# A gated-linear-attention and expert kernel: tokens normalized two tiles at a time, the second output product, its store and the decay sums a step later

## The chip, the core and the metric

The kernel runs on one core of a Trainium2 chip. The engines of the core are TensorE (PE: matmuls, with its weight loads as PEld), VectorE (DVE), ScalarE (ACT), GpSimd (POOL) and SyncE (SP, which here only issues DMAs). Each engine works through its own instructions in the order in which they stand; semaphores make one wait for another. Transfers are made by 16 DMA engines. The metric is the device time of one execution in microseconds (us), and of several runs the median.

## The reference

8192 tokens (4 sequences of 2048) of width 256 are normalized, and two branches are added to the tokens: linear attention with a decay for each head, and a mixture of 64 experts of which each token takes 8.

```python
xn = _layernorm(x, axis=-1)
# attention, 8 heads, DK = 128, DV = 64
q = (x @ Wq); k = (x @ Wk) * DK ** (-0.5); v = (x @ Wv)
alpha = sigmoid((x @ Wg + bg) / 16)
state = at[..., None, None] * state + kt[..., None] * vt[:, :, None, :]
out_t = einsum('bhk,bhkv->bhv', qt, state)
return out * sigmoid(x @ Wog) @ Wo
# experts: groups of 8, the best 4 groups, the best 8 experts, 256 places each
y = einsum('eci,eih->ech', silu(g) * u, w_down)
out = zeros((n, h)).at[token].add(y_slots * w_slot[:, None])
# result
x + attention(xn) + experts(xn)
```

Here `x` inside the two branches is `xn`.

## The kernel before

**Two halves.** Tokens are taken in 32 blocks of 256 (`NS`, two chunks of 128 each) for the attention, and in 16 batches of 512 (`NB`, four tiles of 128) for normalization and routing. A function `block(s)` writes out the attention of block s with twelve calls of `step()` between its parts. In `step()` the side work advances: generators in the list `side`, each with the step at which it starts, run to their next `yield`. In the first half (blocks 0 to 16) these are, one batch to a block, `front(b)` (normalize, part into two half-precision numbers, transpose, routing logits), `back(b)` (choice of experts) and, in groups of batches, `decays(gi)` (sums of the logarithms of the decays). When they are done, from block 17 on, `step()` advances the experts instead, 4.8 to a block: gathers of token rows by POOL (L599), three products, an accumulating scatter by POOL (L677).

**Who sets the order.** The program is written in the order that `block` and `step` give, but a scheduler then orders each engine's instructions by its own reckoning of when they can start. The order of the built program is therefore known, and it differs from the written one.

**A block.** With halves of four heads, block s computes, in the written order: `unit_a(s,0,0)` (the decay matrix: product lp, L864, two activations and the triangle `dc`, L874 on POOL; the scores `sp`), the query product of the second half q10 (`queries(s,1,0)`), the key product k10, then after a step `unit_d(s,0,0)` (product `od`, output `oT`, the new state), the two output products of the block before, here o0 and o1 (`output(s-1,0)` and `output(s-1,1)`, L943 to L947), a step, `finish(s-1)`, then `unit_a(s,0,1)` with its lp, the query product q11, and after a step the key product k11 and the gates (`wog`). Products in half precision are made of three matmuls each (L259, L260, L261): high by high, high by low, low by high. So each result is parted by ACT into a high half (`qh`, `k`, `oh`) and by another engine into a low half (`ql` and `k` at L211 on DVE; `ol` at L935, on POOL in the first half). `qt` (L835, DVE) multiplies a query product by `el`, the decay that SP loads; it is the last to read the query product. `kt` is the transpose of `k` by a DMA that SP issues (L854).

**PSUM.** The query, key, value, gate and output products and lp share one pool of banks, `pj`, taken in turn: 4 banks in the first half, 3 in the second. A product whose bank has not been read by all its readers waits. The routing logits `lg`, `cs`, `ep`, `ltp` and `cp` have the other pool, `mo`.

**front.** For batches from 2 on: statistics by DVE; `rstd` and `nb` by some 14 small POOL operations (L346 to L351); a step later four activations on ACT, one for each tile, in place in `xt` (L362); a step later one cast of all four tiles (L366, ACT) and one subtraction for the low half (L367, POOL), the transposing DMA into `xT` (L370), and the store of the rows (L373); a step later the spill of `xT`, the copy of x to the output and the next batch's load; six steps later `lg`.

**decays.** Logarithm; a step later the sum and its parting into two, `g` (L413, L414); a step later four matmuls for `cs` (L417 to L421), two exponentials and the parting of `cs` into three; a step later the transposes `ep` and `ltp` and the stores to `el_d` and `lt_d`, which later blocks load.

**finish.** For blocks before 17 POOL issues an accumulating DMA of the block's result `res` to the output (L953). From block 17 on ACT issues a plain store to `at_d` (L957), and after each group of blocks (`TOGETHER`: 17 to 20, 21 to 24, 25 to 28, 29 and 30) POOL issues one accumulating DMA of the whole group (L961), in turn with the experts' gathers and scatters.

Of the kernel before, what the change touches and what calls it, by code (L numbers as in the profile page):

```python
# [13 lines left out]
AF = mybir.ActivationFunctionType  # L14
ALU = mybir.AluOpType
# [15 lines left out]
RT = 4  # L31
# [40 lines left out]
def gla_moe_kernel(ctx: ExitStack, tc: tile.TileContext, x, Wq, Wk, Wv, Wo, Wg, bg, Wog,  # L72
                   gate_wT, gate_bias, w_gate, w_up, w_down, out):
    nc = tc.nc
# [239 lines left out]
    def front(b):  # L314

        rows = slice(b * RB, (b + 1) * RB)
        xt = batch[b].pop("xt")
        st = r2.tile([P, RT, 6], F32, name="st")
        mv = r2.tile([P, RT, 2], F32, name="mv")
        for t in range(RT):  # L320
            nc.vector.bn_stats(out=st[:, t, :], in_=xt[:, t, :])
        for t in range(RT):
            nc.vector.bn_aggr(out=mv[:, t, :], in_=st[:, t, :])

        va = r2.tile([P, RT], F32, name="va")
        nc.vector.tensor_scalar(va, mv[:, :, 1], EPS, XFIT ** -2, ALU.add, ALU.mult)
        yi = r2.tile([P, RT], I32, name="yi")
        nc.vector.tensor_scalar(yi, va.bitcast(I32), 1, None, ALU.logical_shift_right)
        rstd = r2.tile([P, RT], F32, name="rstd")
        nc.vector.tensor_scalar(rstd.bitcast(I32), yi, -1.0, float(0x5f3759df), ALU.mult, ALU.add)  # L330
        yield True
        nt = r2.tile([P, RT], F32, name="nt")
        nb = r2.tile([P, RT], F32, name="nb")
        x16 = r1.tile([P, RT, 2, D], F16, name="x16")
        flat = x16.rearrange("p t a d -> p t (a d)")
        xT = r2.tile([P, RT, 2, 2, P], F16, name="xT")
        if b < 2:
            for _ in range(3):
                nc.vector.tensor_tensor(nt, rstd, rstd, ALU.mult)
                nc.vector.scalar_tensor_tensor(nt, in0=nt, scalar=-0.5, in1=va, op0=ALU.mult, op1=ALU.mult)  # L340
                nc.vector.scalar_tensor_tensor(rstd, in0=nt, scalar=1.5, in1=rstd, op0=ALU.add, op1=ALU.mult)
            nc.vector.scalar_tensor_tensor(nb, in0=mv[:, :, 0], scalar=-1.0, in1=rstd,
                                           op0=ALU.mult, op1=ALU.mult)
        else:
            for _ in range(3):
                nc.gpsimd.tensor_tensor(nt, rstd, rstd, ALU.mult)  # L346
                nc.gpsimd.tensor_tensor(nt, nt, va, ALU.mult)
                nc.gpsimd.tensor_scalar(nt, nt, -0.5, 1.5, ALU.mult, ALU.add)
                nc.gpsimd.tensor_tensor(rstd, rstd, nt, ALU.mult)
            nc.gpsimd.tensor_tensor(nb, mv[:, :, 0], rstd, ALU.mult)  # L350
            nc.gpsimd.tensor_scalar(nb, nb, -1.0, None, ALU.mult)  # L351
        if b < 2:
            for t in range(RT):
                made["hi"] = nc.scalar.activation(x16[:, t, 0, :], xt[:, t, :], AF.Identity,
                                                  bias=nb[:, t:t + 1], scale=rstd[:, t:t + 1]).ins
                xn = t5.tile([P, D], F32, tag="t5", name="xn")
                nc.vector.tensor_scalar(xn, xt[:, t, :], rstd[:, t:t + 1], nb[:, t:t + 1], ALU.mult, ALU.add)
                made["xn"] = nc.vector.tensor_tensor(x16[:, t, 1, :], xn, x16[:, t, 0, :], ALU.subtract).ins
        else:
            yield True  # L360
            for t in range(RT):
                nc.scalar.activation(xt[:, t, :], xt[:, t, :], AF.Identity,  # L362
                                     bias=nb[:, t:t + 1], scale=rstd[:, t:t + 1])
            yield True

            nc.scalar.copy(x16[:, :, 0, :], xt)  # L366
            nc.gpsimd.tensor_tensor(x16[:, :, 1, :], xt, x16[:, :, 0, :], ALU.subtract)  # L367
        n = 2 if b == 0 else RT
        for t in range(0, RT, n):
            made["xT"] = nc.sync.dma_start(  # L370
                out=xT[:, t:t + n].rearrange("p t a c i -> p (t a c) i"),
                in_=flat[:, t:t + n].rearrange("p t k -> p (t k)"), transpose=True).ins
        nc.sync.dma_start(out=xw_d[rows, 0:D].rearrange("(t p) d -> p t d", p=P),  # L373
                          in_=flat.bitcast(F32))
        yield True
        stored = nc.sync.dma_start(out=xT_d[b], in_=xT)
        with tc.issue_after(stored.ins):
            nc.sync.dma_start(out=of[rows, :], in_=xf[rows, :])
        batch[b]["xT"] = xT
        if 0 < b < NB - 1:  # L380
            load_x(b + 1)
        for _ in range(6 if b > 2 else 1):
            yield True
        lg = ps["mo"].tile([P, RT, E + H], F32, tag="mo", name="lg")
        for t in range(RT):
            for c in range(2):
                made["lg"] = product(lg[:, t, :], (xT[:, t, 0, c, :], xT[:, t, 1, c, :]),
                                     (gwz[:, 0, c, :], gwz[:, 1, c, :]), c == 0, c == 1)
        nc.vector.scalar_tensor_tensor(zs[:, b].rearrange("p h t -> p t h"), in0=lg[:, :, E:E + H],
                                       scalar=unfit[:, WG:WG + 1], in1=bc(brow, 1, RT),  # L390
                                       op0=ALU.mult, op1=ALU.add)
        nc.scalar.activation(sg[:, b], zs[:, b], AF.Sigmoid)
        sc = r3.tile([P, RT, E], F32, name="sc")
        nc.scalar.activation(sc, lg[:, :, 0:E], AF.Sigmoid, scale=unfit[:, GATE:GATE + 1])
        batch[b]["sc"] = sc
        yield True

    def decays(gi):
# [14 lines left out]
        nc.vector.tensor_scalar(g[:, 0, :], z, CGRID, CGRID, ALU.add, ALU.subtract)  # L413
        made["g"] = nc.vector.tensor_tensor(g[:, 1, :], z, g[:, 0, :], ALU.subtract).ins  # L414
        yield True
        cs = ps["mo"].tile([P, 4, n], F32, tag="mo", name="cs")
        nc.tensor.matmul(cs[:, 0:2, :].rearrange("p a n -> p (a n)"), lhsT=u_le,  # L417
                         rhs=g.rearrange("p a n -> p (a n)"), start=True, stop=True)
# [26 lines left out]
        for i in range(nb_):  # L445
            b = b0 + i
# [437 lines left out]
    def unit_m(s, half, ck):  # L884
        B = blk[s]
        dc = B["dc", half, ck]
        anchor.append(nc.vector.tensor_tensor(dc, B["sp"], dc, ALU.mult).ins)  # L887
# [50 lines left out]
    def output(s, ck):  # L938
        B = blk[s]
        if ck == 0:  # L940
            B["res"] = w2.tile([P, NCK, D], F32, name="res")
        oh_, ol_ = B["oT"][ck]
        rp = ps["pj"].tile([P, D], F32, tag="pj", name="pj")  # L943
        for hp in range(4):
            product(rp, (oh_[:, hp, :], ol_[:, hp, :]),
                    (wparts["wo"][0][:, hp, :], wparts["wo"][1][:, hp, :]), hp == 0, hp == 3)
        nc.scalar.copy(B["res"][:, ck, :], rp)  # L947
# [26 lines left out]
    def block(s):  # L974


        n = s + 1 < NS
        if n:
            load_block(s + 1)
            load_el(s + 1, 0)  # L980
        unit_a(s, 0, 0)
        if n:
            queries(s, 1, 0)
        else:
            keys(s, 1, 0)
        unit_m(s, 0, 0)
        step()
        if n:
            keys(s, 1, 0)
        else:  # L990
            keys(s, 1, 1)
        step()
        unit_d(s, 0, 0)
        if s:
            output(s - 1, 0)
            output(s - 1, 1)
        step()
        if s:
            finish(s - 1)

        unit_a(s, 0, 1)
        queries(s, 1, 1 if n else 0)
        unit_m(s, 0, 1)
        step()
        if n:
            keys(s, 1, 1)
        else:
            queries(s, 1, 1)
        if n:
            load_el(s + 1, 1)  # L1010
            gate(s + 1, 0)
        step()
        unit_d(s, 0, 1)
        step()

        if not n:
            unit_a(s, 1, 0)
            unit_m(s, 1, 0)
            unit_a(s, 1, 1)
            unit_d(s, 1, 0)  # L1020
            split_o(s, 0)
            unit_m(s, 1, 1)
            output(s, 0)
            unit_d(s, 1, 1)
            split_o(s, 1)
            step()
            return
        unit_a(s, 1, 0)
        gate(s + 1, 1)
        unit_m(s, 1, 0)  # L1030
        step()
        values(s + 1, 0)
        queries(s + 1, 0, 0)
        step()
        unit_d(s, 1, 0)
        split_o(s, 0)
        step()

        unit_a(s, 1, 1)
        keys(s + 1, 0, 0)  # L1040
        unit_m(s, 1, 1)
        step()
        queries(s + 1, 0, 1)
        keys(s + 1, 0, 1)
        values(s + 1, 1)
        step()
        unit_d(s, 1, 1)
        split_o(s, 1)
        step()
# [140 lines left out]
```

## Time and profile before

| what | value |
|---|---|
| median of 3 runs | 1230.19 us (1227.66 to 1234.02) |
| profiled execution | 1224.75 us |
| its span, first to last instruction | 1223.0 us |
| mean granted TensorE clock | 0.989 |
| busy: PE, DVE, ACT, POOL | 1134.6, 957.4, 743.8, 725.2 us |
| PE busy from 160 to 200 us, from 640 to 680 us | 38.6 and 40.0 of 40 us |
| HBM | 143 GB/s over the span |

A name such as `pj<-xs,wq_h` says which tile an instruction writes and which it reads. In a list of waits a row tells who waited, who ended the wait, and the time in total, the times and the longest. In the timeline a row has the start, the length, the engine and line, the operation, the tiles, the shapes, and in brackets the idle time of the engine before it with what ended it. A busy PE is not a PE at its peak, since the ends of matmuls are modelled. Weight loads run beside matmuls.

### The profile page before, as it was taken

What the parts mean: (1) busy time and instruction counts of PE and PEld (TensorE: products, weight loads), DVE (VectorE), ACT (ScalarE), POOL (GpSimd) and SP (SyncE); (2) the same over time, 40 slices, a digit from 0 to 9 for tenths busy, and PEclk for the clock granted to TensorE, in tenths of its full rate; (3) what the DMA queues carried; (4) which work ended last, traced back from release to release, by engine and by line L of the source; (5) the groups of instructions that cost most, each with busy time, mean ns of one, the idle gap of its engine ahead of it and who ended that gap; (6) DMA issues with size and microseconds to landing.
All of it is one profiled execution on the core that took longest, in us unless ns stands there. A gap on an engine that the chain in (4) does not pass through costs nothing.

```text
span 1223.0 us, 32182 instructions
## 1 busy us (share of the span) xinstructions
PE 1134.6 (93%) x12409; PEld 959.4 (78%) x12421; DVE 957.4 (78%) x2631; ACT 743.8 (61%) x1394; POOL 725.2 (59%) x892
## 2 busy tenths in 40 slices
PE   3797999988898999999989999999999899999898
PEld 2576877777687787787768888888888788888787
DVE  7978777766678666767878898888889778888775
ACT  4567566666566666644546666656676556665564
POOL 4376677765576677653225665576665647665642
PEclk9999999999999999999999999999999999999899
DMA  7759777687676876655868889889788998988855
GB/s 232 208 138 239 168 178 173 174 170 163 138 176 166 183 181 150 150 104 126 177 120 174 177 178 187 203 179 202 175 198 166 186 156 173 188 177 175 193 77 95
DMA packets 315001, 207.14 MB, mean 169 GB/s; under 512 B 198816, under 2 KB 285728, under 8 KB 314144
## 3 DMA queue, kind: packets, MB, share of 16 engines
q1 hardware_dynamic: 281328, 155.52, 53.9%
q0 software_dynamic: 29712, 45.89, 22.5%
q10 hardware_dynamic: 3808, 3.67, 0.9%
q8 instruction: 97, 1.59, 0.5%
q14 instruction: 56, 0.46, 0.1%
HBM read 115.98 MB, written 58.38 MB: 143 GB/s over the span
## 4 chain that ended last, share of the span: by engine, by line
PE 52%; DVE 15%; DMA 13%; POOL 8%; ACT 6%; issue 4%; SPq 1%; POOLq 0%; DVEq 0%; ACTq 0%
PE pj L261 9%; PE pj L259 9%; PE pj L260 8%; DMA kt<-k 7%; PE od L904 3%; DMA el<-el_d 3%; PE od L908 2%; PE gu L259 2%; PE gu L260 2%; PE gu L261 2%; PE xet L619 2%; DVE qt L835 2%; DVE k L211 1%; ACT xt L362 1%; DVE ql L211 1%
## 5 line engine op out<-in xcount | busy, mean ns | idle before, releaser
L677 POOL DMA_INDIRECT out_dram<-y,idx x128 | 212.5, 1660 | 141.9 <-DMA out_dram<-y,idx 74.6
L599 POOL DMA_INDIRECT xe<-xw_d,idx x128 | 140.4, 1097 | 102.4 <-ACT y L663 31.7
L211 DVE SCALAR_TENSOR_TENSOR ql<-pj,qh 128x512 f16<-128x512 f32 x128 | 87.1, 681 | 68.3 <-ACT qh L210 68.2
L259 PE MATMUL pj<-xs,wk_h 128*128 128x256 f16 x496 | 135.9, 274 | 1.7 <-ACT og L802 1.7
L260 PE MATMUL pj<-xs,wk_h 128*128 128x256 f16 x496 | 135.6, 273 | 0.0
L261 PE MATMUL pj<-xs,wk_l 128*128 128x256 f16 x496 | 135.6, 273 | 0.0
L259 PE MATMUL pj<-xs,wq_h 128*128 128x256 f16 x496 | 135.3, 273 | 0.2 <-DVE k L211 0.2
L261 PE MATMUL pj<-xs,wq_l 128*128 128x256 f16 x496 | 135.3, 273 | 0.0
L260 PE MATMUL pj<-xs,wq_h 128*128 128x256 f16 x496 | 135.3, 273 | 0.0
L887 DVE TENSOR_TENSOR dc<-sp,dc 128x512 f32<-128x512 f32 x128 | 87.4, 683 | 39.2 <-POOL dc L874 31.2
L904 PE MATMUL od<-dc,v 128*64 128x128 f32 x1024 | 107.7, 287 | 7.4 <-DVE dc L887 6.5
L210 ACT ACTIVATE k<-pj 128x512 f16<-128x512 f32 x128 | 76.2, 596 | 43.5 <-PE pj L261 43.2
L210 ACT ACTIVATE qh<-pj 128x512 f16<-128x512 f32 x128 | 76.3, 596 | 40.1 <-PE pj L261 39.7
L908 PE MATMUL od<-qt,state 128*64 128x128 f32 x960 | 98.6, 274 | 0.0
L259 PE MATMUL sp<-qh,k 128*128 128x128 f16 x512 | 96.8, 223 | 0.7 <-ACT k L210 0.2
L261 PE MATMUL sp<-qh,k 128*128 128x128 f16 x512 | 96.4, 223 | 0.8 <-DVE k L211 0.6
L260 PE MATMUL sp<-ql,k 128*128 128x128 f16 x512 | 96.2, 222 | 0.4 <-DVE ql L211 0.4
L211 DVE SCALAR_TENSOR_TENSOR k<-pj,k 128x512 f16<-128x512 f32 x128 | 86.6, 677 | 6.7 <-ACT k L210 6.6
L917 DVE SCALAR_TENSOR_TENSOR oT<-og,od 128x256 f32<-128x256 f32 x128 | 52.9, 413 | 46.6 <-PE od L261 44.4
L663 ACT ACTIVATE y<-yp,xe 128x256 f32<-128x256 f32 x128 | 53.6, 470 | 58.3 <-PE yp L261 52.8
L835 DVE SCALAR_TENSOR_TENSOR qt<-pj,el 128x512 f32<-128x512 f32 x128 | 86.7, 678 | 1.5 <-DMA el<-el_d 1.5
L868 ACT ACTIVATE dc<-lp 128x512 f32<-128x512 f32 x128 | 76.5, 598 | 18.6 <-PE lp L864 16.8
(397 smaller groups left out, 4242.2 us busy)
## 6 DMA issues: line engine op xcount, KB each, us to landing
el<-el_d SPq DMA_DIRECT2D x64, 512.0 KB
xw_d<-x SPq DMA_DIRECT2D x16, 512.0 KB
xT_d<-xT SPq DMA_DIRECT2D x16, 512.0 KB
out_dram<-in_L_attn_x_dram SPq DMA_DIRECT2D x16, 512.0 KB
w<-in_L_ffn_w_gate_dram SPq DMA_DIRECT2D x64, 128.0 KB
w<-in_L_ffn_w_up_dram SPq DMA_DIRECT2D x64, 128.0 KB
w<-in_L_ffn_w_down_dram SPq DMA_DIRECT2D x64, 128.0 KB
xs<-xT_d SPq DMA_DIRECT2D x31, 256.0 KB
```

Source lines behind the costliest of these rows:

```text
L210: return (nc.scalar.activation(hi, t, AF.Copy, scale=scale).ins, nc.vector.scalar_tensor_tensor(lo, in0=t, scalar=scale, in1=hi, op0=ALU.m ...
L211: nc.vector.scalar_tensor_tensor(lo, in0=t, scalar=scale, in1=hi, op0=ALU.mult, op1=ALU.subtract).ins)
L259: nc.tensor.matmul(out_, lhsT=a[0], rhs=b[0], start=first, stop=False)
L260: nc.tensor.matmul(out_, lhsT=a[0], rhs=b[1], start=False, stop=False)
L261: return nc.tensor.matmul(out_, lhsT=a[1], rhs=b[0], start=False, stop=last).ins
L599: in_turn(lambda: nc.gpsimd.indirect_dma_start(out=xe[:, f, :], out_offset=None, in_=xw_d[:, :], in_offset=bass.IndirectOffsetOnAxis(ap=id ...
L677: two = [in_turn(lambda: nc.gpsimd.indirect_dma_start(out=of, out_offset=bass.IndirectOffsetOnAxis(ap=idx[:, e, f:f + 1], axis=0), in_=m[" ...
L835: read = nc.vector.scalar_tensor_tensor(qt, in0=pj, scalar=QFIT, in1=two_heads(el, i), op0=ALU.mult, op1=ALU.mult)
L868: nc.scalar.activation(dc, lp, AF.Relu, scale=-1.0)
L887: anchor.append(nc.vector.tensor_tensor(dc, B["sp"], dc, ALU.mult).ins)
L904: nc.tensor.matmul(op[i * DV:(i + 1) * DV, j, :], lhsT=v[:, h0 + 2 * j + i, :], rhs=dc[:, 2 * j + i, :], start=True, stop=first)
L908: nc.tensor.matmul(op[i * DV:(i + 1) * DV, j, :], lhsT=state[half][:, 2 * j + i, :], rhs=qt[:, ck, 2 * j + i, :], start=False, stop=True)
```

## The change

Four edits. In `front` the normalization goes two tiles at a time: in one step the activations of tiles 0 and 1, in the next those of tiles 2 and 3 together with the cast and the subtraction of tiles 0 and 1, in the third the cast and the subtraction of tiles 2 and 3, then the transposing DMA and the row store. Cast and subtraction are thus two instructions each instead of one, and all that follows them is a step later; `lg` stays in its step for batches from 3 on, because one of the six steps ahead of it goes. In `decays` a further step stands between `g` and `cs` for every group but the first. In `block` the second output product is made after the second `unit_m`, behind lp and q11, and `finish` after it.

```diff
         else:
-            yield True
-            for t in range(RT):
-                nc.scalar.activation(xt[:, t, :], xt[:, t, :], AF.Identity,
-                                     bias=nb[:, t:t + 1], scale=rstd[:, t:t + 1])
-            yield True
-
-            nc.scalar.copy(x16[:, :, 0, :], xt)
-            nc.gpsimd.tensor_tensor(x16[:, :, 1, :], xt, x16[:, :, 0, :], ALU.subtract)
+
+            for t in range(0, RT + 2, 2):
+                yield True
+                if t < RT:
+                    for t2 in range(t, t + 2):
+                        nc.scalar.activation(xt[:, t2, :], xt[:, t2, :], AF.Identity,
+                                             bias=nb[:, t2:t2 + 1], scale=rstd[:, t2:t2 + 1])
+                if t:
+                    ts = slice(t - 2, t)
+                    nc.scalar.copy(x16[:, ts, 0, :], xt[:, ts])
+                    nc.gpsimd.tensor_tensor(x16[:, ts, 1, :], xt[:, ts], x16[:, ts, 0, :], ALU.subtract)
...
-        for _ in range(6 if b > 2 else 1):
+        for _ in range(5 if b > 2 else 1):
             yield True
...
         yield True
+        if gi:
+            yield True
         cs = ps["mo"].tile([P, 4, n], F32, tag="mo", name="cs")
...
         if s:
             output(s - 1, 0)
-            output(s - 1, 1)
         step()
-        if s:
-            finish(s - 1)
 
         unit_a(s, 0, 1)
         queries(s, 1, 1 if n else 0)
         unit_m(s, 0, 1)
+        if s:
+            output(s - 1, 1)
+            finish(s - 1)
         step()
```

## The prediction

> **What bounds the kernel now.** I read the page first, then PE's waits, then the timeline where the longest of them end, then the transfers and the granted clock by stretch.
>
> The page's busy list:
>
> ```profile
> PE 1134.6 (93%) x12409; PEld 959.4 (78%) x12421; DVE 957.4 (78%) x2631; ACT 743.8 (61%) x1394; POOL 725.2 (59%) x892
> ```
>
> PE is the bound: 88 us of the span are idle, 34 of them in the first 120 us. The change adds no matmul, so it can only move PE's waits. The longest of them (who waited, us in total, times, longest):
>
> ```profile
> PE od L259 <- DMA kt<-k: 21.4, 9, 5.0
> PE lg L259 <- DMA xT<-x: 11.0, 3, 9.8
> PE pj L259 <- DVE qt L835: 10.3, 5, 3.8
> ...
> PE pj L261 <- POOL ol L935: 7.0, 7, 1.7
> ...
> PE cs L417 <- DVE g L414: 3.5, 3, 1.7
> ```
>
> The change aims at three of these: ol (block boundaries of the first half, tokens with routing), qt (the same half), cs. The timeline at a boundary (start, length, instruction, idle before it):
>
> ```profile
> 185.47 1.27 POOL L935 TENSOR_TENSOR ol<-oT,oh 128x512 fp32r<-128x512 f32 x1
> ...
> 186.71 0.68 DVE L835 SCALAR_TENSOR_TENSOR qt<-pj,el 128x512 f32<-128x512 f32 x1
> 186.79 0.39 PE L261 MATMUL pj<-wo_h,ol 128*128 128x256 f32 x1 [0.87 <-POOL ol L935]
> ```
>
> The second output product (o1) waits for POOL's low half; qt, 0.6 us behind, has no PE work waiting yet. Both long qt waits come from ACT:
>
> ```profile
> 322.82 2.07 ACT L362 ACTIVATE xt<-xt,nb,rstd 128x256 f32<-128x256 f32 x4 [2.08 <-POOL nb L351]
> 324.91 1.28 ACT L869 ACT_TABLE_LOAD   x1
> 326.21 0.63 ACT L869 ACTIVATE dc<-dc 128x512 f32<-128x512 f32 x1
> 326.74 0.58 ACT L210 ACTIVATE qh<-pj 128x512 f16<-128x512 f32 x1
> ```
>
> Four normalizations stand ahead of qh. PE, waiting for the pj bank that qt releases, sat idle for 3.82 us until 328.70. In the second half (experts) PE waits for kt alone:
>
> ```profile
> 941.66 0.93 POOL L961 DMA_DIRECT2D out_dram<-at_d  x1 [4.47 <-DVE le__16521 L586]
> ...
> 946.26 8.83 SPq L854 DMA_TRANSPOSE kt<-k  x1
> ...
> 960.23 0.24 PE L259 MATMUL od<-vwh,kt 128*128 128x64 f16 x1 [4.69 <-DMA kt<-k]
> ```
>
> **Second output product, first half.** In the order of the changed program's instructions o1 stands behind lp and the query product q11, so ol has 0.2 + 12 x 0.109 = 1.5 us more; the seven waits are 0.5 to 1.66, so the 7.0 go. But the four pj banks are taken in turn: before, o1 and lp lie between the query products q10 and q11, and lp takes q10's bank, a product later. Now the turn is q10, k10, o0, lp, q11, and q11 takes q10's bank, which qt releases last. At this boundary o0 starts at 184.01, its 12 matmuls of 0.117 and lp end at 185.65, and q11 waits until 187.45: 1.8 us in place of 0.87. From there q11 (1.31) and o1 (1.42) end at 190.18, against 189.63 before. At six boundaries qt's end less the end of the ol wait is 0.37, 0.60, 0.62, 0.10, 1.24 and 0.07 us: the new wait is about 1.5 each, 0.5 longer than the old. I charge 1.5 at twelve boundaries (blocks 3 to 14): +18. It is zero wherever qt is early, as at 15 and 16.
>
> **Two tiles at a time.** Each of 14 batches gets one more ACT cast and one more POOL subtraction. The nearest rows of half size are vwh and vwl (616 and 1216 ns) against 1037 and 2185 for the whole: 14 x 0.20 = 2.7 us of ACT and 14 x 0.25 = 3.5 us of POOL, hidden by idle shares of 39% and 41%; uncovered they would add at most those 6 us. What matters is order: in most blocks the built order still has the four normalizations together, but behind qh of q11, also where the two long waits were (3.16 and 3.82). In three blocks they stand ahead of qh; there q11 is earlier by o1 (1.4 us), and I leave 0.7 us each. All 10.3 us of qt waits go, and one stretch of half clock: 3.4 us at 0.50, so 1.7.
>
> The transposes, the row store, the spill, the copy of x and the next load come a step later on SP, in the old places relative to kt in most blocks. The next load has over six steps (some 16 us) against a transfer of about 5. Cost nothing; if a load were late, the front alone would slip.
>
> **Sums of log decays.** cs leaves the wait for g by standing behind a product: of 3.5 us 0.5 stay, and the 0.9 us wait of ltp behind it goes. Its DMAs to el_d and lt_d come a step later; block 8 first needs them at 316, they were stored from 255 on.
>
> **The store and the adds.** finish is behind o1. In the first half POOL's accumulate issue (1.28 us) waits for res behind ACT's normalizations, and the state product (L926) and the subtraction queue behind it. The state product ran at 161.00 for a DVE add at 166.89, so some 2 us later is covered; without cover each microsecond goes to the next block's od. In the second half the ACT-issued store and POOL's 1 MB add (L961, three of them, and one of half that size) move past lp and q11: 1.5 us. The gathers queued behind the add were issued 17 us or more before their use, so nobody waits. At the tail the last add waited for expert adds until 1209 anyway; a store landing 1.5 us later costs 0 to 1.
>
> What changes is the add's lead over kt. It was issued 4.6 us before kt at 941.66, and 3.2 us before kt at 1123.29. While it ran, the transfers by queue read:
>
> ```profile
> q0 software_dynamic: 211, 1.31, 87.4%
> q1 hardware_dynamic: 138, 0.28, 11.5%
> ```
>
> (stretch 943 to 951: packets, MB, share of 16 engines; kt is in q1). So kt waited for the add almost whole, and two waits of 4.69 and 4.98 came with 10.2 us of half clock, 5.1 lost: 14.8 in all are at stake. A lead shorter by 1.5 us lets el and the rest ahead of kt move before the add: I take 1.5 for each of the two, -3. The bounds are 0 and -14.8 (kt wholly ahead), and +1.5 each if the add merely ends later.
>
> The Trainium skill says otherwise of such a pair ("DMA: Bandwidth & Descriptors", Queues, rings and completion order): a DMA engine takes the queues it has work for in turn, a packet each. By that kt would share evenly, the lead would hardly matter, and this term would be 0. The 11.5% speaks against it here.
>
> **Sum.** Gone: ol 7.0, qt 10.3, cs and ltp 3.9, half clock 1.7, and of the 1.65 of block 16's wait for res all (that bank now comes from lp): 24.5. New: 18 + 2.1 for the three blocks = 20.1. First half -4.4; with -3 for the adds -7.4. The profiled execution took 1224.75 us (span 1223.0 and 1.75 around it), 0.4% under the median of 1230.19 (runs 1227.66 to 1234.02). Against its own time this is 1217.3; against the median, which I forecast, 1222.8.
>
> **The rivals.**
>
> *kt passes the adds.* From o1's end to the end of the key product before kt, PE has in the old order 7.2 and 7.7 us of work for the two waits, in the new 1.5 and 3.6. If the small difference lets kt go first, all 14.8 go instead of 3: 1211. Against it: el and xs are still ahead of kt in its queue. 0.16.
>
> *The wait only changes its name.* At the boundaries the chain table load, exp, qh, ql, qt is the limit, whichever PE instruction waits for it; if the long qt waits return as waits of lp or the gate and the adds stay, only cs and little else remains: -1.5, 1228.7. For it: 18 of 24.5 come back in my own sum. 0.24.
>
> *The bank wait decides, slower.* qt's chain begins with lg, which PE itself delivers, so a late PE makes the next qt late. If q11 waits 2.4 us, not 1.5, at the twelve boundaries, that is +11. It turns at 2.1 us a boundary, where the gain is gone. Waits of that size also reach the clock: the kt wait of 2.35 us at 983.28 was followed by a granted clock of 0.50, those for ol of 1.42 and 1.66 by none:
>
> ```profile
> 983.50:986.90 3.40, 3.40 (x31) 3.31 (x28) 1.58 (x5) 0.68 (x2) 2.27 (x2) 0.50 0.55 155
> 415.00:421.00 6.00, 4.58 (x38) 4.11 (x37) 2.58 (x4) 4.00 (x8) 4.24 (x13) 1.00 0.44 93
> ```
>
> (stretch, its length, busy time of the five engines, granted clock.) With four such stretches at 1.7 it is +18 in all: 1241. 0.20.
>
> The skill ("TensorE: Matmul & The Clock Gate", Part 1) has the clock halved only after an idle window of some 3.4 us; by it the last 7 us would not come. The stretch after 983.28 disagrees.
>
> **How the numbers follow.** My forecast has 0.40, and within it 1215 to 1228. 0.5%, 6.15 us, is about what a measurement can tell from no change: faster means under 1224.0. Of the forecast 0.31 lies there, with the first rival 0.47; the second rival and 0.09 of the forecast give 0.33; the third 0.20. The range takes in the first rival and most of the third: 1209 to 1238; the likeliest case's own is 1215 to 1228.
>
> **What would show it.** Right: no PE wait for ol in the first half, in its place waits of wq's pj for DVE qt of 1 to 2 us, some twelve; no wait of the gate over 2 us; cs under 1 us; L362's wait for nb much as before (28.6), its normalizations still four in a row; the kt waits at the adds of blocks 25 and 29 shorter. Wrong: waits of q11 above 2 us with half clock in the first half, new kt waits elsewhere in the second, or POOL's state product late enough for od to wait for DVE's state.

## The result and the profile after

The changed kernel takes 1235.8 us (median of 22 runs, 1230.5 to 1242.4); the kernel before takes 1228.1 us beside it (22 runs, 1217.1 to 1239.3). The ratio is 1.0081 with a 95% interval of 1.0061 to 1.0101: 0.8% slower. The ratio is taken over fast runs alone, so it is not quite the quotient of the two medians. The profiled execution took 1238.24 us, its span 1236.5.

The page's busy list after:

```profile
PE 1140.6 (92%) x12408; PEld 960.1 (78%) x12421; DVE 979.0 (79%) x2631; ACT 745.9 (60%) x1408; POOL 728.8 (59%) x906
```

DVE does the same 2631 instructions as before in 21.6 us more. That is the line to keep in mind. PE's waits after (us in total, times, longest):

```profile
PE pj L259 <- DVE qt L840: 18.7, 14, 1.9
PE od L259 <- DMA kt<-k: 16.1, 11, 3.4
...
PE od L909 <- DVE dc L892: 9.3, 5, 3.6
...
PE sp L261 <- DVE k L211: 6.5, 10, 1.2
PE cp L519 <- DVE sel L514: 4.5, 9, 0.8
...
PE cs L422 <- DVE g L417: 1.4, 1, 1.4
```

The waits for ol and the long waits of the gate's product for qt are gone. In their place stand the waits for the bank that qt releases, 14 times. Three more rows grew: `od` waiting for dc, `sp` for k's low half and `cp` for `sel`, all made by DVE. The waits for kt are fewer us over the whole span, but more in the first half: 6.7 us between blocks 2 and 16, where the kernel before has 3.9.

Where the time went, by stages (a stage begins with DVE's first `dc<-sp,dc` of the block):

| stage | before | after |
|---|---|---|
| start to block 2 | 117.6 us | 123.5 us |
| block 2 to block 16 | 452.1 | 466.7 |
| block 16 to block 30 | 591.1 | 570.9 |
| block 30 to the end | 62.3 | 75.4 |

From block 2 to 16 PE is idle 37.7 us in place of 28.5, and the records show it at half clock for 20.4 us in place of 6.8; of that it was busy 19.5 against 6.2 us, so half of the difference, 6.7 us, is lost work. The first stage is not steady: with unchanged code two of the experiments below, e3 and e8, have 118.8 and 121.8.

The boundary of block 4 after, beside the one that the prediction shows (start, length, instruction, idle before it):

```profile
192.39 0.63 ACT L874 ACTIVATE dc<-dc 128x512 f32<-128x512 f32 x1
...
192.93 0.58 ACT L210 ACTIVATE qh<-pj 128x512 f16<-128x512 f32 x1
...
194.14 0.68 DVE L840 SCALAR_TENSOR_TENSOR qt<-pj,el 128x512 f32<-128x512 f32 x1
...
194.88 0.28 PE L259 MATMUL pj<-xs,wq_h 128*128 128x256 f16 x1 [1.93 <-DVE qt L840]
```

q11 waits 1.93 us for qt, where the 0.87 us wait for ol stood. Behind this wait the clock was halved. Four stretches behind bank waits of 1.93, 1.94, 1.93 and 1.92 us (the column behind the five engines is the granted clock):

```profile
195.10:198.50 3.40, 3.40 (x18) 2.83 (x17) 1.30 (x3) 1.32 (x4) 1.84 (x8) 0.50 0.00 0
229.20:232.60 3.40, 3.40 (x18) 2.92 (x17) 1.52 (x4) 1.55 (x4) 1.63 (x7) 0.50 0.00 0
466.00:469.40 3.40, 3.40 (x37) 3.13 (x36) 2.19 (x4) 2.11 (x5) 1.77 (x7) 1.00 0.00 0
```

In the first two PE ran 18 matmuls, in the third 37 in the same time. The fourth, at 499.50, was at 1.00 too. The records show what parts them. In each trace the clock changes only on lines 3.413 us apart (here 195.09, 198.51, 229.22, 317.97), and PE's idle time between two lines tells the clock behind the second. From 60 us on in this trace, 1.88 us of idle time or more between two lines was followed by 0.50, and 1.83 us or less by 1.00. The two waits that ended at 465.77 and 499.26 were parted by such a line, into 0.90 and 1.03 us and into 1.54 and 0.38 us. In the 20 traces together the most that left the clock at 1.00 is 1.98 us, and the least that lowered it 1.68 us (the ends of matmuls are modelled).

**Why DVE takes longer.** Groups of DVE instructions between block 2 and block 16 (busy us, then mean ns of one), before:

```profile
L465 DVE TENSOR_TENSOR h<-sfc 128x128 f32<-128x128 f32 x14 | 6.5, 466 | 0.0
L472 DVE TENSOR_TENSOR h<-h 128x64 f32<-128x64 f32 (+1 forms) x28 | 5.5, 196 | 0.0
L466 DVE TENSOR_TENSOR l<-sfc 128x128 f32<-128x128 f32 x14 | 3.9, 279 | 0.0
```

and after:

```profile
L477 DVE TENSOR_TENSOR h<-h 128x64 f32<-128x64 f32 (+1 forms) x28 | 14.8, 529 | 0.0
...
L471 DVE TENSOR_TENSOR l<-sfc 128x128 f32<-128x128 f32 x14 | 12.9, 923 | 0.0
L470 DVE TENSOR_TENSOR h<-sfc 128x128 f32<-128x128 f32 x14 | 11.3, 806 | 0.0
```

These small maxima and minima of the routing (`back`) have the same shapes and counts and take 39.0 us in place of 15.9, while others got shorter (the sum of all DVE instructions grew by 16.8). The timeline of DVE, POOL and PE in block 13 after shows what they meet:

```profile
505.74 3.53 DVE L471 TENSOR_TENSOR l<-sfc 128x128 f32<-128x128 f32 x1
...
505.80 1.08 POOL L931 TENSOR_TENSOR state<-state,wall 128x256 f32<-128x256 f32 x1
...
506.38 2.72 POOL L370 TENSOR_TENSOR x<-xt,x 128x512 f16<-128x512 f32 x2
...
509.93 0.68 DVE L211 SCALAR_TENSOR_TENSOR k<-pj,k 128x512 f16<-128x512 f32 x1
...
510.67 0.23 PE L261 MATMUL sp<-qh,k 128*128 128x128 f16 x1 [1.24 <-DVE k L211]
```

The minimum, 0.28 us when it stands alone, takes 3.53 us and ends at 509.27, 0.17 us after POOL's two subtractions have ended (509.10). Behind it on DVE the remaining routing and the low half of k stand, which ACT's part had left ready at 506.29; PE waits for it. In the same block before, the two did not meet:

```profile
487.62 0.28 DVE L466 TENSOR_TENSOR l<-sfc 128x128 f32<-128x128 f32 x1
...
492.05 2.12 POOL L367 TENSOR_TENSOR x<-xt,x 128x1024 f16<-128x1024 f32 x1
```

The Trainium skill describes this ("SBUF — State Buffer", SBUF: two separate sides): a VectorE operation with two SBUF inputs and a GpSimd operation that reads SBUF take turns at one shared pair of ports as a lock, held for a whole instruction, and the other blocks. The trace agrees: the minimum ended only when POOL's subtractions had, and it was long beside three POOL instructions in a row.

**Why kt is late in the first half.** SP issues its DMAs one after the other, too. Block 7 after, the end of a kt wait:

```profile
306.41 4.10 SPq L373 DMA_TRANSPOSE xT<-x  x1
...
307.08 0.68 DVE L211 SCALAR_TENSOR_TENSOR k<-pj,k 128x512 f16<-128x512 f32 x1
...
310.60 3.90 SPq L859 DMA_TRANSPOSE kt<-k  x1
...
316.63 0.20 PE L259 MATMUL od<-vwh,kt 128*128 128x64 f16 x1 [2.44 <-DMA kt<-k]
```

k was whole at 307.76, but SP was busy with `front`'s transposing DMA until 310.51, and kt was issued only then. It is the same in blocks 2, 6 and 10 (k ready 6.1, 4.1 and 3.6 us ahead of kt): these four make 5.8 of the 6.7 us. Before, kt went ahead of xT in blocks 2 and 10; in blocks 6 and 7 it stood behind it, for waits of 0.5 us and none.

**The second half.** The add of blocks 21 to 24 and the kt next to it, after (before, the add was issued 4.6 us ahead of kt):

```profile
965.11 3.68 SPq L859 DMA_TRANSPOSE kt<-k  x1
...
969.50 0.94 POOL L966 DMA_DIRECT2D out_dram<-at_d  x1 [4.79 <-DVE hs L646]
```

kt now goes first, and PE's wait of 4.69 us there is gone. But the add is issued 14.5 us into block 25 in place of 8.2, the next 24.0 us into block 29 in place of 9.7; the gathers and scatters that stand behind the adds on POOL come later too. When block 30 starts, 55 of 64 experts have been scattered, against 58. The scatters go out in pairs 6 to 9 us apart. The last links of the chain of waits after:

```profile
1221.36 3.67 DMA out_dram<-y,idx
...
1225.22 2.67 DMA mo<-out_dram
...
1227.99 0.42 DVE mo L975
```

The last expert scatter starts at 1221.36 (1204.75 before), and only behind it can the last block's rows be read back. So 20.2 us gained up to block 30 are followed by 13.1 lost: -7.1 in all. Part of both is only work moved across the line: PE had made the last product of 57.3 experts when block 30 started, against 59.0, and from there to the end it is busy 63.3 us in place of 56.7.

### The profile page after: what moved, and what is told of

The parts are those of the page before. It is cut to its first block, busy times and chain, and to the rows that moved or that the text cites. A ratio compares the mean times of both kernels' runs of the same rounds, so it can differ in the third digit from the quotient of the medians.

```text
span 1236.5 us, 32193 instructions
## 1 busy us (share of the span) xinstructions
PE 1140.6 (92%) x12408; PEld 960.1 (78%) x12421; DVE 979.0 (79%) x2631; ACT 745.9 (60%) x1408; POOL 728.8 (59%) x906
## 3 DMA queue, kind: packets, MB, share of 16 engines
q0 software_dynamic: 29712, 45.89, 21.6%
## 5 line engine op out<-in xcount | busy, mean ns | idle before, releaser
L682 POOL DMA_INDIRECT out_dram<-y,idx x128 | 215.4, 1683 | 114.5 <-DMA out_dram<-y,idx 57.4
L604 POOL DMA_INDIRECT xe<-xw_d,idx x128 | 142.9, 1116 | 112.7 <-ACT y L668 66.7
L259 PE MATMUL pj<-xs,wq_h 128*128 128x256 f16 x496 | 137.6, 277 | 18.1 <-DVE qt L840 18.1
L260 PE MATMUL pj<-xs,wq_h 128*128 128x256 f16 x496 | 137.4, 277 | 0.0
L909 PE MATMUL od<-dc,v 128*64 128x128 f32 x1024 | 109.6, 288 | 10.2 <-DVE dc L892 9.3
L696 DVE TENSOR_TENSOR wl<-w,wh 128x768 fp32r<-128x768 f32 x64 | 61.1, 955 | 37.9 <-ACT wh L628 37.8
L909 PEld LDWEIGHTS od<-dc,v 128*64 128x64 f32 x1024 | 60.3, 137 | 36.1 <-DVE dc L892 11.2
```

Source lines behind the costliest of these rows:

```text
L259: nc.tensor.matmul(out_, lhsT=a[0], rhs=b[0], start=first, stop=False)
L260: nc.tensor.matmul(out_, lhsT=a[0], rhs=b[1], start=False, stop=False)
L604: in_turn(lambda: nc.gpsimd.indirect_dma_start(out=xe[:, f, :], out_offset=None, in_=xw_d[:, :], in_offset=bass.IndirectOffsetOnAxis(ap=id ...
L682: two = [in_turn(lambda: nc.gpsimd.indirect_dma_start(out=of, out_offset=bass.IndirectOffsetOnAxis(ap=idx[:, e, f:f + 1], axis=0), in_=m[" ...
L696: eng.tensor_tensor(lo, full, hi, ALU.subtract)
L909: nc.tensor.matmul(op[i * DV:(i + 1) * DV, j, :], lhsT=v[:, h0 + 2 * j + i, :], rhs=dc[:, 2 * j + i, :], start=True, stop=first)
```

## The experiments

All edits are to the kernel before, if nothing else is said. "Block 16" is the time at which block 16 starts in the profile (before 569.6, after 590.2). "DVE sum" is the length of all DVE instructions between blocks 2 and 16, added up from the trace (before 388.4, after 405.2 us).

**The edits one by one.** e1 has only the block edit (o1 and `finish` behind q11), e2 only the pairs of tiles, e4 only the decays' step, each as in the change's diff. e3 has the block edit with one condition:

```diff
+        late = s >= 18
         if s:
             output(s - 1, 0)
-            output(s - 1, 1)
+            if not late:
+                output(s - 1, 1)
...
         unit_m(s, 0, 1)
+        if s and late:
+            output(s - 1, 1)
+            finish(s - 1)
```

> The kernel before with the block edit alone (second output product o1 and finish behind lp and q11, in all blocks). Bank theory (the loss of the first half is q11's wait for the bank that qt releases, some 14 waits of 1.2 to 1.9 us, and the half clock that the longest of them bring): ol waits gone, bank waits there as in the changed kernel, time +5 to +12 us against before. Front theory (the loss comes from the normalization in pairs): the block edit is neutral or a small gain, -7 to +2 us, though the bank waits are there too. Tail theory (the loss is made behind block 30, where the last adds come later): block 16 starts as early as before, the last PE instruction some 8 us later against block 30.

> The kernel before with the front edit alone (normalization, cast and subtraction two tiles at a time, one step less ahead of lg). Bank theory: no new bank wait of q11, the ol waits stay (7 us), the long qt waits of the gate (10.3 us) go or shrink: -8 to 0 us. Front theory: +5 to +15 us, with block 16 starting 8 us or more later than before and new waits for kt, dc and the low half of k in blocks 2 to 16. Tail theory: 0 within 3 us.

> The kernel before with the block edit only in blocks 18 to 31, where experts run. Bank theory: the second half's gain without the first half's loss, -5 to -15 us if the shorter kt waits of the changed kernel's profile are the edit's work, 0 if they are chance. Front theory: likewise -5 to 0. Tail theory: +5 to +10 us, since the last blocks are changed as in the changed kernel.

> The kernel before with the one further step ahead of the decay sums alone. All theories: the wait of cs for g (3.5 us) falls to 0.5 to 1.5 us, -1 to -3 us in that stage, time -3 to +2 us. If it is over +4 us, the order that the scheduler finds for the rest moves the time, and none of the three edits' own mechanisms.

| run | ratio to before, 95% interval | block 16 | DVE sum |
|---|---|---|---|
| e1 | 1.0192 (1.0154 to 1.0230) | 588.9 | 405.5 |
| e2 | 1.0028 (0.9996 to 1.0061) | 572.2 | 390.9 |
| e3 | 1.0033 (0.9998 to 1.0067) | 566.5 | 386.9 |
| e4 | 1.0031 (1.0001 to 1.0061) | 566.1 | 387.5 |

The block edit alone brings the whole loss of the first half, and the longer DVE sum with it, though its subtraction is still one of four tiles; the pairs alone bring neither. e1 is more than any theory asked (+23.8 us; the bank theory had +5 to +12), and so is e4 by a little (+4.6 by the medians, forecast -3 to +2). e1's median is 14.6 us over that of the full change, although block 16 starts as late and the order of PE, ACT and DVE in the second half is all but the same in both. In the two profiles 8.9 us of this arise between blocks 18 and 30, 5.3 of them idle time of PE; why stays open, and with it how the three edits add up to the time of the changed kernel. e3 shows the second half's edit to be no gain (+4.5 by the medians): block 30 to the end took 74.9 us, the add in block 29 came at 24.0.

**Which part of the block edit.** e5 moves only `finish`, e6 both output products, e7 the block edit with `finish` behind k11 and kt, all in blocks 1 to 17; e8 has the block edit in blocks 18 to 25. In short, without the condition that takes `finish` out of its old place:

```diff
# e5
         unit_m(s, 0, 1)
+        if s and s < 18:
+            finish(s - 1)
# e7
         if n:
             keys(s, 1, 1)
+            if s and s < 18:
+                with tc.issue_after(made["kt"]):
+                    finish(s - 1)
```

> The kernel before with only finish moved behind q11, in blocks 1 to 17; both output products stay where they were. The loss of the first half with the block edit is some 19 us (e1 less e3). Bank theory: no bank wait of q11 on the query product before it, so -2 to +3 us. Collision theory (finish's accumulating transfer is issued 2 to 5 us ahead of the transpose kt in place of 6 to 8 and slows it, so that od waits for kt): kt waits of the first half 8 us or more against 3.7, +8 to +19 us.

> Both output products and finish behind q11, in blocks 1 to 17 only. Now lp takes a bank and q11 the next, as before the change, and no product comes to the bank of q10 within a product of it. Bank theory: no bank wait of q11 over 1 us, no wait for ol, time -10 to 0 us against before. Collision theory: finish comes as late as with the block edit or later, kt waits 8 us or more in the first half, +8 to +19 us.

> The block edit in blocks 1 to 17 only, with finish a further place later, behind the key product k11 and the issue of its transpose kt. The bank waits of q11 stay, the accumulating transfer no longer runs ahead of kt. Bank theory: +12 to +20 us, as with the block edit. Collision theory: kt waits of the first half back at 4 us or less, time 0 to +6 us.

> The block edit in blocks 18 to 25 only, with the adds of two groups of blocks (17 to 20, 21 to 24) in it; the last blocks are as before. Tail theory (in e3 the add in block 29 comes 24 us into the block in place of 10, the experts' gathers and scatters behind it come later, 9 experts in place of 6 are still to be scattered at block 30, and the end waits for them): 6 or 7 scatters left at block 30, block 30 to the end 62 to 66 us in place of 75, time 5 to 12 us under e3, so -7 to 0 us against before. If the loss lay in the blocks themselves: as e3, +2 to +6 us.

| run | ratio to before, 95% interval | block 16 | DVE sum |
|---|---|---|---|
| e5 | 0.9984 (0.9952 to 1.0015) | 568.8 | 392.6 |
| e6 | 1.0093 (1.0062 to 1.0124) | 579.3 | 398.4 |
| e7 | 1.0141 (1.0098 to 1.0184) | 587.8 | 406.2 |
| e8 | 0.9991 (0.9958 to 1.0024) | 570.6 | 389.2 |

`finish` costs nothing (e5), and putting its transfer behind kt saves nothing (e7: kt waits 12.5 us from block 2 to 16): the collision theory falls. e6 has the time and the kt waits that it asked (+9.4 and 10.6 us), but 9.4 of these again stand behind xT. The bank waits did not go there: o0, now the fourth product behind q10, took q11's place in the wait (13 waits for qt from 110 to 620 us, 17.1 us in all). e8 has the time and the tail that the tail theory asked (62.8 us from block 30 to the end), with 56.5 experts scattered there, just short of the 57 or 58 forecast. But e7, which has no edit behind block 17, has the late add as well (29.3 us into block 29, 77.7 us from block 30 to the end), and so has e9 below, which also takes only 568.5 us from block 16 to 30. So gain and lag of the second half can come without any edit there. The adds stand in the same place among POOL's gathers and scatters in these kernels as before (118 gathers and 108 scatters ahead of the third); what comes later in e7 are the experts as a whole, with 56.0 of them through their last product at block 30 against 59.0. An edit upstream can tip the order that the scheduler finds for them.

**The bank wait taken away.** e9 is the block edit in blocks 1 to 17 (e3's diff with `s < 18`). e10 adds to it, and e12 to the changed kernel, a bank of the other pool for the lp ahead of q11; e11 is the changed kernel with the block edit undone.

```diff
-        lp = ps["pj"].tile([P, 4, P], F32, tag="pj", name="lp")
+        own = s < 18 and (half, ck) == (0, 1)
+        lp = ps["mo" if own else "pj"].tile([P, 4, P], F32, tag="mo" if own else "pj", name="lp")
```

> The block edit in blocks 1 to 17 only. Bank theory (the loss lies in the first half, where o1 now stands behind q11): block 16 starts some 19 us later than before (569.6), as in e1 and e7, time +12 to +20 us. Tail theory (most of the loss is made behind block 17): 0 to +6 us.

> As e9, but in blocks 0 to 17 the decay product lp that stands between o0 and q11 takes a bank of the other PSUM pool (mo), so that q11 has a bank to itself and o1, a product of 1.3 us later, takes the bank of q10. Bank theory: the waits of wq's and wo's pj for DVE qt fall from 13 to 17 us to under 6, block 16 starts 8 us or more earlier than in e9 (580 or less), time 6 us or more under e9. Rival (the chain of ACT and DVE behind the query product is the limit, whichever PE instruction waits for it): the waits go to lp, sp or od under another name, block 16 within 4 us of e9.

> The changed kernel with the block edit undone: normalization in pairs and the further step of the decays together. Bank theory: block 16 starts at 565 to 573, time 0 to +6 us against before, as e2 and e4 alone, and so 2 to 10 us under the changed kernel. If the pairs and the decays are a gain only where the block edit is (the changed kernel took 14 us less than e1): the same, 0 to +6. If they are a gain by themselves: -8 to -3 us.

> The changed kernel, with lp of the first half in the other pool as in e10. Bank theory: q11's waits for DVE qt go from 17 us to under 6, block 16 starts at 580 or less in place of 590, time 6 us or more under the changed kernel: within 4 us of before. Rival (chain the limit): within 4 us of the changed kernel, +5 to +12 us against before.

| run | ratio to before, 95% interval | block 16 | DVE sum |
|---|---|---|---|
| e9 | 1.0097 (1.0063 to 1.0131) | 588.2 | 406.8 |
| e10 | 1.0299 (1.0251 to 1.0347) | 608.7 | 395.5 |
| e11 | 1.0032 (1.0009 to 1.0056) | 569.9 | 394.8 |
| e12 | 1.0213 (1.0171 to 1.0256) | 599.4 | 403.0 |

e11 closes the account of the first half: without the block edit it is as fast as before. e9 has block 16 where the bank theory put it, and +11.6 us, just under its +12 to +20. e10 (+42.6) and e12 (+26.8) lie beyond what either theory asked. PE's waits of e12 between blocks 2 and 16:

```profile
PE od L259 <- DMA kt<-k: 12.4, 5, 4.5
PE od L910 <- DVE dc L893: 6.7, 8, 2.7
...
PE pj L259 <- ACT oh L940: 4.3, 4, 1.9
PE pj L259 <- DVE qt L840: 3.4, 7, 0.7
```

The waits for qt fell from 18.1 us (the same view of the changed kernel) to 3.4, yet PE is idle for 38.9 us in this stage, against 37.7. So the bank theory falls as the whole account of the loss: take that wait away in this manner, and kt, dc and oh stand in its place. It is not a clean test, since lp now shares a pool with `lg`, `cs`, `ep` and `ltp`, and e10 went further astray (23.5 us of waits for oh, 6.0 of ltp for DVE).

**o1's work and o1's place.** e13 leaves out three of o1's four head pairs in its old place; e14 leaves o1 out; e15 and e16 put it behind k11 and behind the gate, all in blocks 1 to 17; e17 is e15 from block 3 on, e18 is e17 with the change's other two edits.

```diff
# e13, in output
-        for hp in range(4):
+        heads = range(1) if ck and s < 17 else range(4)
+        for hp in heads:
# e15
             keys(s, 1, 1)
+            if s and late:
+                output(s - 1, 1)
+                finish(s - 1)
```

> The kernel before with three of o1's four head pairs left out in the blocks that blocks 1 to 17 output (9 of 12 matmuls, 1.0 us each time; the second chunk of those blocks is not the full product). Order and bank turn are those of before. Up to block 16 some 15 us of PE work are gone. Cover theory (o1 stands in time in which PE waits anyhow for qt): block 16 starts 0 to 7 us earlier than before (562 to 570), and waits of pj or lp for DVE qt come in o1's place. Work theory (PE bound by its work): 12 us or more earlier (558 or less).

> The kernel before with o1 left out in blocks 1 to 17 (the second chunk is given o0's product instead): one bank fewer is taken, so q11 takes q10's bank as in the changed kernel. 21 us of PE work are gone up to block 16. Cover theory: q11 waits for qt as in the changed kernel, block 16 within 8 us of before (562 to 578), so that with o1's own 21 us behind q11 the 588 of e9 come out. Work theory: block 16 at 555 or less.

> o1 and finish behind the key product k11 in blocks 1 to 17, one product further than in the block edit. Cover theory: o1 costs its full length there too, block 16 at 583 to 592, +10 to +20 us. Place theory (right behind q11 it delays k11 and so kt, dc and the low half of k; behind k11 it delays none of them): block 16 at 565 to 577, time -5 to +6 us.

> o1 and finish behind the gate's product, directly ahead of the next od, in blocks 1 to 17. There PE waited for dc and kt in the changed kernel, 3 to 10 us in the first half. Cover theory: block 16 at 580 to 590, the bank waits of q11 as in the changed kernel. Place theory: block 16 at 565 to 575, kt and dc waits of the first half under 4 us, time -6 to +5 us.

> As e15, but o1 and finish stand behind k11 only in blocks 3 to 17; blocks 1 and 2 are as before, since e15 lost 9.5 us there and from block 2 to 16 took as long as before (451.7 against 452.1). Place theory: block 16 at 566 to 573, waits of the first half for kt, the low half of k and sel together under 5 us though q11's bank waits stay at 10 us or more; time -5 to +5 us against before. If any place behind q11 costs the time: +6 to +12.

> As e17, with the other two edits of the change added, the normalization in pairs and the further step of the decays: the changed kernel with its o1 one product further behind from block 3, and in its old place in blocks 1, 2 and 18 to 31. Place theory: -6 to +5 us against before, some 5 to 10 us under the changed kernel. If the pairs or the decays cost time by themselves (e2, e4 and e11 each +3 to +4): +3 to +8.

| run | ratio to before, 95% interval | block 16 | DVE sum |
|---|---|---|---|
| e13 | 0.9979 (0.9946 to 1.0012) | 572.6 | 389.1 |
| e14 | 0.9737 (0.9689 to 0.9785) | 547.3 | 387.4 |
| e15 | 1.0085 (1.0043 to 1.0128) | 578.8 | 391.0 |
| e16 | 1.0052 (1.0021 to 1.0083) | 582.5 | 397.0 |
| e17 | 1.0042 (1.0006 to 1.0079) | 579.4 | 390.1 |
| e18 | 1.0123 (1.0073 to 1.0173) | 586.6 | 401.3 |

e13 has the cover theory's time: 9 matmuls of 12 less in each block, no time gained. From block 2 to 16 PE is busy 416.0 us in place of 423.6 and idle 38.7 in place of 28.5. But the sign that the theory named did not come: the waits for qt are 8.7 us there (8.3 before), and the new idle time is spread over ltp, dc, oh and others. e14 speaks against it: without o1 the first half is 22 us shorter, as the work theory had it, and q11 waits for qt 2.4 us only, though it takes q10's bank as in the changed kernel. e14's order on ACT differs as well (at the boundary of block 4 qh stands ahead of a table load that in the kernel before stands ahead of qh), so the two runs don't decide between work and chain; that stays open. e15 to e17 show that o1 behind k11 or the gate is no better than ahead of lp: e15 and e16 come out between the two theories (+11.1 and +8.2 us), and in e17 block 16 starts later than the place theory's 566 to 573. e18 loses more than either theory asked (+14.1 us), and more than e17 and e11 together. In e17 the waits for k's low half and sel are down to 0.9 us and those for kt to 5.2 (14.2 in e9), near what the place theory asked, and DVE is undisturbed, but others came; PE's waits between blocks 2 and 16:

```profile
PE pj L259 <- DVE qt L835: 14.4, 10, 1.9
PE od L904 <- DVE dc L887: 9.1, 7, 3.8
PE od L259 <- DMA kt<-k: 5.2, 3, 3.0
```

No version beat the kernel before but e14, which does less; e2, e3, e5, e8 and e13 (which does less, too) are equal to it within their intervals.

**What the runs settle.** In all kernels with o1 ahead of lp, whole or thinned (before, e2, e3, e4, e5, e8, e11, e13), block 16 starts at 566 to 573; in all with o1 behind q11 at 579 to 609. So o1's place costs the first half its time: shown. How it does so is read from the traces, and has several parts. With o1 right behind q11 (after, e1, e7, e9) the DVE sum is 405 to 407 in place of 387 to 395, and blocks 2 to 16 take 465 to 468 us in place of 448 to 455. In these kernels 23 to 27 us of DVE's excess length (the instruction less the shortest of its form) lie beside POOL's subtraction L367 (L370 after), against 7.0 before; and kt waits behind xT for 5.8 us after and for 12 to 14 us in e1, e7 and e9. Further behind (e15 to e17) the DVE sum is 390 to 397 and the loss smaller, 0 to 10 us in that stage, by the bank and dc waits.

That the meeting of DVE and POOL is what costs the time is not shown. Two runs speak against it as the whole: e6 has 27.1 us of excess beside the subtraction and loses only 7.6 us from block 2 to 16, and e10 has none (0.0) and is the slowest of all. A kernel that takes the subtraction off POOL, or kt out from behind xT, with the block edit kept was not run.

## Why the prediction was wrong, step by step

**Second output product.** The bank wait was forecast with its place, cause and size: 20.1 us in all, measured 18.7, longest 1.94; the 7.0 us of ol and the 10.3 us of the gate's waits went as forecast, and cs left one wait of 1.4. By those terms alone (18.7 less 7.0, 10.3 and 2.1) idle time would have stayed about the same, -0.7. What failed is what this step left out. It asked where q11 would wait, and not what the work that q11 and o1 delay would then meet on the other engines. kt, k's low half, sel and dc brought 11.7 us more of waits over 0.4 us between blocks 2 and 16 (18.4 against 6.7), nowhere in the sum; e1, with this edit alone, has 23.9.

**Two tiles at a time.** The extra instructions were hidden, as forecast, and the edit itself costs nearly nothing (e2 and e11: +0.3%). The ground given for it, "hidden by idle shares of 39% and 41%", is the weak point, and it matters for the block edit: POOL's idle share says nothing of whom POOL holds up while it works. Its subtraction stood beside DVE's routing instructions that were up to 12.6 times as long as alone (3.53 us against 0.28). The halves were not needed for it (e1, e7 and e9 have the whole subtraction); it was enough that the block edit moved the two to the same time. The same holds for SP: "in the old places relative to kt in most blocks" and "Cost nothing" left out the four blocks in which xT now holds kt up, and e1 and e9 have these waits without this edit.

**Half clock.** Forecast 1.7 us gained, measured 6.7 lost from block 2 to 16. The third rival had 7 for this, with four stretches behind bank waits of 2.4 us. Bank waits of 1.93 and 1.94 us brought two stretches of 3.4 us; the longest, 6.8 us, stands behind a wait of 2.47 us for dc, and another behind a kt wait of 2.44. That the rival's figure came out is luck. The prediction also counted half of each stretch as lost, idle time included: at the adds PE was busy in 6.7 of the 10.2 us, which makes 3.4 lost and not 5.1.

**The adds.** -3 was taken for shorter kt waits; at blocks 25 and 29 they went from 4.69 and 4.98 to none and 0.50, the first rival's event at block 25, where kt went first, while others of 3.37 and 3.29 stand at blocks 16 and 21. From block 16 to 30 all kt waits together fell from 17.5 to 8.3 us. The gain was larger and the step after it wrong: "a store landing 1.5 us later costs 0 to 1" at the tail. The add was not 1.5 but 6 to 14 us later in its block, the experts behind it lagged by three, and the tail took 13.1 us more. The net, -7.1 in the profiles, is near the forecast by two errors that cancel, and e3 shows no gain. Nor does the share of 11.5% settle whether the queues were served in turn: the same lines count 211 packets of about 6.2 KB and 138 of about 2.0 KB, so by packets kt's queue was not far behind.

**Sum.** First half: -4.4 forecast, +20.6 at block 16 in the profiles: +5.9 before block 2 (where 4.2 lie between runs with unchanged code), +9.2 idle and about +5.5 of longer PE work behind it. Of the rivals the third had the sign and nearly the time (1241), but little of its mechanism: bank waits of 2.4 us did not occur, and half of the added half clock stands behind other waits. The signs named as "wrong" (half clock in the first half, new kt waits elsewhere in the second) were the ones that came.

## What to carry to other kernels

Before a product is moved on a bound engine, follow what it delays and ask what that will now coincide with: here GpSimd's long subtraction and VectorE's short two-input operations, which before the change met less often, and on SP one transposing DMA that holds up the next. An engine's idle share does not make work on it free. Look up whose instructions grow longer while it runs, by comparing the mean length of one in groups of the same shape. And a wait removed on a chain that is nearly balanced comes back under another name (e12: 15 us of bank waits gone, no time gained), so count the idle of the whole stage and not one row.

## What the runs showed of the hardware

- A VectorE minimum with two SBUF inputs of 128 x 128 took 0.28 us alone and 3.53 us beside three GpSimd instructions in a row, ending 0.17 us after the subtractions.
- The granted clock changed only on lines 3.413 us apart. After the change, idle time of TensorE of 1.88 us or more between two lines was followed by 0.50, and of 1.83 us or less by 1.00; so a wait of 1.94 us within a step halved the clock, and one of 1.92 us parted by a line did not.
- SyncE's transposing DMAs held each other up: kt was issued 2.8 to 6.1 us after its data was ready, behind xT, in four blocks after the change.
- Leaving out 9 of 12 matmuls of a product in 17 blocks (e13) changed neither the time (0.9979, 0.9946 to 1.0012) nor the start of block 16 for the better.
- Edits that end at block 17 (e7) moved the add in block 29 from 9.7 to 29.3 us into the block.
